# Spike counts accumulated by TensorE in PSUM, and two instead of three tiles for gathered rows

## The chip, the cores and the metric

The kernel runs on one core of one Trainium2 chip. The metric is the device time in microseconds (us) of one execution. The engines are called as the profile calls them: PE (TensorE matmuls; PEld is its weight loads), DVE (VectorE), ACT (ScalarE), POOL (GpSimd) and SP (SyncE).

## The reference

A table of 100001 embeddings of 128 numbers is read at 1024 x 50 positions. For each of 50 steps the running mean of a sequence's rows is normalised over the batch of 1024 and fed to a leaky integrator, whose state v gives off a spike when it reaches 1. The mean number of spikes is multiplied by the whole table.

```python
emb = emb_table.at[0].set(0.0)
e = emb[seq]                                   # (1024, 50, 128)
prefix = jnp.cumsum(e, axis=1)
denom = jnp.minimum(t_idx[None, :], lengths[:, None])
uF = prefix / denom[:, :, None]
y = (uF - uF.mean(axis=0)) * lax.rsqrt(uF.var(axis=0) + BN_EPS) * gamma + beta
def step(v, x):                                # 50 steps
    v = v + (x - v) / 2.0
    spike = (v - 1.0 >= 0)
    return v - spike, spike
_, spikes = lax.scan(step, v0, jnp.moveaxis(y, 1, 0))
scores = spikes.mean(axis=0) @ emb.T           # (1024, 100001): 410 MB
```

## The kernel before

Two stages follow each other: the recurrence over t, then the product with the table, whose 410 MB of results are stored. In the recurrence D = 128 lies on the partitions and the batch on the free axis. Rows are gathered by POOL, 128 rows to an indirect DMA, eight of them to a step (the batch of 1024):

```python
gp = ph.enter_context(tc.tile_pool(name="gather", bufs=3))

def gather(t):
    es[t] = gp.tile([P, B], F32, tag="e", name=f"e_{t}")
    for n in range(NB):                       # NB = 8
        nc.gpsimd.indirect_dma_start(
            out=es[t][:, n * P : (n + 1) * P],
            out_offset=None,
            in_=table,
            in_offset=bass.IndirectOffsetOnAxis(ap=idx[:, n, t : t + 1].bitcast(U32), axis=0),
        )
```

PE transposes them and adds them up in the PSUM banks `pre`; DVE takes the mean and the statistics; ACT scales; DVE does the integrator and counts the spikes:

```python
for t in range(T):                            # T = 50
    last = t == T - 1
    if t + 1 < T:
        gather(t + 1)
    e = es.pop(t)
    # ... (last: s and negv, see below, are made here)
    for h, cs in enumerate(halves):
        for k in range(0, BANK, P):
            nc.tensor.matmul(pre[h][:, k : k + P], lhsT=e[:, ...], rhs=ident, is_transpose=True, ...)
        nc.vector.scalar_tensor_tensor(uF[:, cs], rlen[:, cs], 1.0 / (t + 1), pre[h], ALU.max, ALU.mult)
        nc.vector.bn_stats(bs[:, h, :], uF[:, cs])
    if not last:
        correct(t + 1, l)                     # 2 matmuls into pre, for rows of index 0
    # ... bn_aggr, sqrt and scaling on ACT, five small DVE operations for a
    if t and not last:
        nc.vector.tensor_single_scalar(s, v, V_TH, ALU.is_ge)
    # ...
    if not last:
        x(whole)                              # ACT
        if t:
            nc.vector.tensor_tensor(negv, s, v, ALU.subtract)
        step(whole)                           # DVE: v = -0.5 negv + x
        v = vt
        if t < T - 2:
            spiked(count, whole, v)           # DVE: count = (v >= 1) + count
        # ...
        if T - 8 <= t < T - 2 and t % 2 == 0:
            q = (t - T + 8) // 2
            prepare(0, q, accp.tile([P, HALF], F32, tag="pt", name=f"pt_{q}"))
```

`prepare` transposes a piece of 1024 table rows and splits it into a high and a low part for the product stage. Seven chunks of the table (2 MB each) are loaded at the start, while the recurrence runs. In the product stage each tile of results, 128 x 4096, is stored with one DMA of 2 MB.

## Time and profile before

| | before |
|---|---|
| median of the first 3 runs | 1593.33 us (1592.67 to 1593.39) |
| the profiled execution | 1677.8 us, span 1676.0 us |
| busy, share of the span | PE 63%, DVE 60%, ACT 38%, POOL 23% |
| recurrence, up to the first store | 597.4 us of the profiled span |
| product and stores | 1078.6 us of the profiled span |

The profiled execution was 84.5 us slower than the timed ones. The view of the kernel before in 40 equal slices of 41.9 us gives busy tenths for each engine, then the granted clock of PE and the DMA engines' share in tenths:

```profile
PE   3222322322233378887877887887887878888885
DVE  4677777767776875545555555554555555555553
POOL 7666666666666300000000000000000000000000
PEclk6555555555555589999999999999999999999998
DMA  9311111111111069999999999999999999999998
```

From the third slice to the 14th DVE is busy six to eight tenths and the DMA engines one tenth or less (the 9 and the 3 before them are loads of the table). POOL stands at six tenths. From slice 16 on the DMA engines are full. The chain of work that ended last, by engine:

```profile
DMA 49%; DVE 29%; another core or an unknown queue 7%; PE 7%; ACT 3%; issue 3%; POOL 0%; DVEq 0%; SPq 0%; ACTq 0%
```

### The profile page before, as it was taken

The page shows a single profiled execution, that of the slowest core. Times are in us where ns is not written, and L with a number is a line of the kernel's source. Part 1 is how long each engine was busy: PE and PEld are TensorE (multiplying, and loading weights), DVE is VectorE, ACT ScalarE, POOL GpSimd, SP SyncE. Part 2 cuts the span into 40 slices and gives each one's busy share as a digit, 9 for nine tenths or more (in the row PEclk, how much of TensorE's full clock was granted, in tenths as well). Part 3 has the DMA queues.
Part 4 walks back from the last instruction along what each step waited for, and adds up shares of the span by engine and source line. Part 5 has one row for each costly group of instructions (what it writes and reads, how often), then busy time and mean ns, then how long its engine had stood idle before and what let it go on. Part 6 is the DMA issues. An engine that isn't in the chain of part 4 may idle for free.

```text
span 1676.0 us, 12554 instructions
## 1 busy us (share of the span) xinstructions
PE 1047.9 (63%) x4434; PEld 797.5 (48%) x4434; DVE 999.2 (60%) x1211; ACT 630.2 (38%) x697; POOL 378.3 (23%) x406
## 2 busy tenths in 40 slices
PE   3222322322233378887877887887887878888885
PEld 2111212212222266665666665666665666666664
DVE  4677777767776875545555555554555555555553
ACT  2222222222222244444444444444444444444452
POOL 7666666666666300000000000000000000000000
PEclk6555555555555589999999999999999999999998
DMA  9311111111111069999999999999999999999998
GB/s 341 107 46 46 45 48 48 48 44 49 46 45 46 28 271 419 426 425 419 426 417 419 416 417 417 420 424 414 415 416 415 420 416 423 420 410 418 415 413 352
DMA packets 58411, 488.14 MB, mean 291 GB/s; under 512 B 12491, under 2 KB 13292, under 8 KB 33772
## 3 DMA queue, kind: packets, MB, share of 16 engines
q1 hardware_dynamic: 35728, 424.57, 60.2%
q10 hardware_dynamic: 9820, 36.52, 6.0%
q0 software_dynamic: 12800, 26.24, 5.4%
q8 instruction: 35, 0.57, 0.1%
q14 instruction: 28, 0.23, 0.0%
HBM read 77.69 MB, written 409.60 MB: 291 GB/s over the span
## 4 chain that ended last, share of the span: by engine, by line
DMA 49%; DVE 29%; another core or an unknown queue 7%; PE 7%; ACT 3%; issue 3%; POOL 0%; DVEq 0%; SPq 0%; ACTq 0%
DMA scores<-o 48%; DVE o L403 6%; PE po L148 6%; DVE bs L294 4%; DVE uF L293 4%; DVE v L325 4%; DVE count L263 3%; DVE s L308 3%; DVE negv L330 2%; ACT o L405 2%; ACT v L322 1%; DVE a L316 1%; DMA e<-in_L_rec_emb_table,idx 1%; DVE lo L136 1%
## 5 line engine op out<-in xcount | busy, mean ns | idle before, releaser
L403 DVE TENSOR_SCALAR o<-po 128x1024 f32<-128x1024 f32 x390 | 462.1, 1219 | 448.3 <-DMA scores<-o 356.4
L405 ACT ACTIVATE o<-po 128x1024 f32<-128x1024 f32 (+1 forms) x390 | 384.6, 1018 | 548.3 <-DMA scores<-o 380.9
L187 POOL DMA_INDIRECT e<-in_L_rec_emb_table,idx x400 | 377.6, 944 | 189.3 <-issue 109.5
L148 PE MATMUL po<-hi,countC 128*128 128x512 f32 x784 | 325.7, 416 | 90.0 <-ACT o L405 89.7
L252 PE MATMUL pre<-zT,l 128*128 128x512 f32 x100 | 77.7, 779 | 386.6 <-DVE uF L293 333.9
L148 PE MATMUL po<-lo,countC 128*128 128x512 f32 x784 | 311.5, 398 | 0.0
L148 PE MATMUL po<-hi,countB 128*128 128x512 f32 x588 | 246.9, 420 | 32.7 <-ACT o L405 32.2
L148 PE MATMUL po<-lo,countB 128*128 128x512 f32 x588 | 239.5, 408 | 0.0
L252 PEld LDWEIGHTS pre<-zT,l 128*128 128x128 f32 x100 | 28.8, 289 | 428.8 <-issue 312.8
L148 PEld LDWEIGHTS po<-hi,countC 128*128 128x128 f32 x784 | 150.7, 192 | 151.7 <-ACT o L405 123.0
L148 PEld LDWEIGHTS po<-lo,countC 128*128 128x128 f32 x784 | 150.9, 193 | 27.9
L302 ACT ACTIVATE r<-mv,eps 128x1 f32<-128x1 f32 x50 | 14.8, 295 | 388.5 <-DVE mv L298 229.6
L103 PE MATMUL pt<-ident,rows 128*128 128x128 f32 x782 | 110.0, 286 | 80.9 <-ACT o L405 74.6
L148 PEld LDWEIGHTS po<-hi,countB 128*128 128x128 f32 x588 | 117.5, 200 | 71.8 <-ACT o L405 42.2
L136 DVE TENSOR_TENSOR lo<-pt,hi 128x1024 fp32r<-128x1024 f32 x98 | 117.3, 1216 | 55.3 <-ACT hi L132 55.2
L103 PEld LDWEIGHTS pt<-ident,rows 128*128 128x128 f32 x782 | 92.7, 146 | 107.1 <-ACT o L405 92.8
L293 DVE SCALAR_TENSOR_TENSOR uF<-rlen,pre 128x512 f32<-128x512 f32 x100 | 67.8, 678 | 122.4 <-remote 109.7
L148 PEld LDWEIGHTS po<-lo,countB 128*128 128x128 f32 x588 | 117.2, 199 | 23.6
L132 ACT CAST hi<-pt 128x1024 fp32r<-128x1024 f32 x98 | 98.9, 1009 | 50.8 <-PE pt L103 41.8
L284 PE MATMUL pre<-ident,e 128*128 128x128 f32 x400 | 98.0, 420 | 8.3 <-DMA e<-in_L_rec_emb_table,idx 6.9
L284 PEld LDWEIGHTS pre<-ident,e 128*128 128x128 f32 x400 | 83.9, 222 | 20.4 <-issue 10.5
L148 PE MATMUL po<-hi,countA 128*128 128x512 f32 x194 | 76.6, 395 | 1.1 <-ACT o L405 1.1
(61 smaller groups left out, 679.5 us busy)
## 6 DMA issues: line engine op xcount, KB each, us to landing
scores<-o SPq DMA_DIRECT2D x190, 2048.0 KB
rows<-in_L_rec_emb_table ACTq DMA_DIRECT2D x17, 2048.0 KB
rows<-in_L_rec_emb_table SPq DMA_DIRECT2D x7, 2048.0 KB
scores<-o SPq DMA_DIRECT2D x8, 848.5 KB
e<-in_L_rec_emb_table,idx POOLq DMA_INDIRECT x400
scores<-o SPq DMA_DIRECT2D x2, 1024.0 KB
scores<-o SPq DMA_DIRECT2D x3, 512.0 KB
scores<-o SPq DMA_DIRECT2D x2, 256.0 KB
```

Source lines behind the costliest of these rows:

```text
L103: nc.tensor.transpose(pt[:, k0 : k0 + kw], rows[c][:kw, q * KQ + k0 // P, :], ident[:kw, :kw])
L132: nc.scalar.copy(vh, vp)
L136: nc.vector.tensor_tensor(vl, vp, vh.bitcast(F32), ALU.subtract)
L148: nc.tensor.matmul(po[:, :kw], lhsT=counts[n], rhs=part[:, k0 : k0 + kw], start=j == 0, stop=j == 1,)
L187: nc.gpsimd.indirect_dma_start(out=es[t][:, n * P : (n + 1) * P], out_offset=None, in_=table, in_offset=bass.IndirectOffsetOnAxis(ap=idx[: ...
L252: nc.tensor.matmul(pre[h], lhsT=l, rhs=zT[:, h * BANK : (h + 1) * BANK], start=t == 0, stop=False, skip_group_check=True,)
L284: nc.tensor.matmul(pre[h][:, k : k + P], lhsT=e[:, h * BANK + k : h * BANK + k + P], rhs=ident, start=False, stop=last, is_transpose=True, ...
L293: nc.vector.scalar_tensor_tensor(uF[:, cs], rlen[:, cs], 1.0 / (t + 1), pre[h], ALU.max, ALU.mult)
L294: nc.vector.bn_stats(bs[:, h, :], uF[:, cs])
L325: nc.vector.scalar_tensor_tensor(vt[:, cs], negv[:, cs], -0.5, vt[:, cs], ALU.mult, ALU.add)
L403: nc.vector.tensor_scalar_mul(o[:, h0 : h0 + hw], po[:, :hw], 1.0 / T)
L405: nc.scalar.mul(o[:, h0 : h0 + hw], po[:, :hw], 1.0 / T)
```

## The change

The intent is to take work off DVE, the busiest engine of the recurrence. The spikes `s` are there anyway, as bf16 zeros and ones. PE multiplies them by the identity and adds the result up in two PSUM banks over 49 steps; DVE's count operation goes. To find those two banks, the pieces prepared during the recurrence now use the banks of `v`. The tiles for gathered rows go from three to two. This is the diff, cut to its core:

```diff
-        gp = ph.enter_context(tc.tile_pool(name="gather", bufs=3))
+        gp = ph.enter_context(tc.tile_pool(name="gather", bufs=2))
...
-        count = once.tile([P, B], F32, tag="count", name="count")
-        nc.vector.memset(count, 0.0)
+        ident_h = once.tile([P, P], BF16, tag="ident_h", name="ident_h")
+        nc.vector.tensor_copy(ident_h, ident)
...
+        sums = [accp.tile([P, BANK], F32, tag=f"sums{h}", name=f"sums{h}") for h in range(B // BANK)]
...
+        def counted(t, s):
+            for h in range(B // BANK):
+                nc.tensor.matmul(
+                    sums[h],
+                    lhsT=ident_h,
+                    rhs=s[:, h * BANK : (h + 1) * BANK],
+                    start=t == 0,
+                    stop=t == T - 2,
+                    skip_group_check=True,
+                )
...
             if not last:
                 correct(t + 1, l)
+            else:
+                counted(t - 1, s)
+                count = once.tile([P, B], F32, tag="zT", name="count")
+                for h, cs in enumerate(halves):
+                    nc.scalar.copy(count[:, cs], sums[h])
...
                 nc.vector.tensor_single_scalar(s, v, V_TH, ALU.is_ge)
+                counted(t - 1, s)
...
-                if t < T - 2:
-                    spiked(count, whole, v)
...
-                    prepare(0, q, accp.tile([P, HALF], F32, tag="pt", name=f"pt_{q}"))
+                    prepare(0, q, vp.tile([P, HALF], F32, tag="v1", name=f"pt_{q}"))
...
-        spiked(count, whole, v)
```

(Not shown: the first block of the product stage takes `sums` and the banks of `v` in another order.)

More of the change, by code (lines that the diff above doesn't have):

```diff
@@ L339, in rec_kernel @@
                     q = (t - T + 8) // 2
-                    prepare(0, q, accp.tile([P, HALF], F32, tag="pt", name=f"pt_{q}"))
-        pt = accp.tile([P, HALF], F32, tag="pt", name="pt_3")
+                    prepare(0, q, vp.tile([P, HALF], F32, tag="v1", name=f"pt_{q}"))
+        pt = vp.tile([P, HALF], F32, tag="v0", name="pt_3")
         turned(0, 3, pt)
@@ L365, in rec_kernel @@
         for q in range(1, 4):
-            o = (up if q == 3 else gp).tile([P, HALF], F32, tag="uF" if q == 3 else "e", name=f"o_0_0_{q}")
-            po = (accp if q % 2 == 0 else vp).tile(
-                [P, HALF], F32, tag="v0" if q % 2 else "pt", name=f"po_0_0_{q}"
-            )
-            for k0 in range(0, HALF, BANK):
-                product(po[:, k0 : k0 + BANK], 0, q, 0, k0, BANK)
+            pool, tag = (gp, "e") if q == 1 else (up, "uF")
+            o = pool.tile([P, HALF], F32, tag=tag, name=f"o_0_0_{q}")
+            if q == 1:
+                po = sums
+            else:
+                po = vp.tile([P, HALF], F32, tag=f"v{(q + 1) % 2}", name=f"po_0_0_{q}")
+                po = [po[:, cs] for cs in halves]
             for h, cs in enumerate(halves):
-                if h == 0:
-                    nc.scalar.mul(o[:, cs], po[:, cs], 1.0 / T)
-                else:
-                    nc.vector.tensor_scalar_mul(o[:, cs], po[:, cs], 1.0 / T)
+                product(po[h], 0, q, 0, h * BANK, BANK)
+            nc.scalar.mul(o[:, :BANK], po[0], 1.0 / T)
+            nc.vector.tensor_scalar_mul(o[:, BANK:], po[1], 1.0 / T)
             store(0, q * HALF, o)
```

## The prediction

> **What bounds the kernel now.** I read the busy shares and the 40 slices first, then the stretches, the groups of the recurrence, and the order of time of one step. The slices show two stages: until about 590 us the clock granted to PE is half and the DMA engines are nearly idle (the 50 steps of the recurrence); after that the DMA engines are full (the product and its stores). The sums by stretch, with engines as busy (xinstructions) and then granted clock, DMA share and GB/s:
>
> ```profile
> 60.60:568.10 507.50, 152.06 (x474) 104.21 (x474) 377.67 (x634) 131.77 (x183) 339.53 (x360) 0.51 0.16 47
> ...
> 597.40:1676.00 1078.60, 871.12 (x3883) 676.90 (x3881) 574.37 (x492) 478.34 (x487) 0.00 (x0) 0.97 0.99 414
> ```
>
> The second stretch starts at the first store. DMA is at 0.99 there, and the change leaves its bytes alone, so its 1078.6 us stay. The first stretch is what can move. Its groups, 100 to 540 us:
>
> ```profile
> L187 POOL DMA_INDIRECT e<-in_L_rec_emb_table,idx x309 | 291.5, 943 | 150.0 <-issue 83.9 <-remote 47.9 <-PE pre L252 11.2
> ...
> L263 DVE SCALAR_TENSOR_TENSOR count<-v,count 128x1024 f32<-128x1024 f32 x38 | 46.5, 1224 | 1.5
> ```
>
> DVE is the busiest engine in the recurrence, and the count is one of its long operations. But busy time is not the pace. In order of time (start, duration, engine):
>
> ```profile
> 303.78 0.94 POOL L187 DMA_INDIRECT e<-in_L_rec_emb_table,idx  x1 [0.30 <-issue]
> 304.85 1.22 DVE L263 SCALAR_TENSOR_TENSOR count<-v,count 128x1024 f32<-128x1024 f32 x1
> 305.02 0.94 POOL L187 DMA_INDIRECT e<-in_L_rec_emb_table,idx  x1 [0.30 <-issue]
> 305.99 0.68 DVE L293 SCALAR_TENSOR_TENSOR uF<-rlen,pre 128x512 f32<-128x512 f32 x1
> ...
> 313.60 1.22 DVE L263 SCALAR_TENSOR_TENSOR count<-v,count 128x1024 f32<-128x1024 f32 x1
> ...
> 314.74 0.68 DVE L293 SCALAR_TENSOR_TENSOR uF<-rlen,pre 128x512 f32<-128x512 f32 x1
> ```
>
> A step of DVE without a wait is 314.74 - 305.99 = 8.75 us. A gather is 0.94 us and 0.30 us of issue, one each 1.248 us, and a step needs eight: 9.98 us. **POOL's gathers are slower than DVE's step by 1.23 us even with the count in it.** The trace nevertheless averages 11.3 us a step, because of pauses like this, where DVE and POOL stop together:
>
> ```profile
> 91.37 1.91 PE L284 MATMUL pre<-ident,e 128*128 128x128 f32 x8
> ...
> 104.73 0.69 DVE L293 SCALAR_TENSOR_TENSOR uF<-rlen,pre 128x512 f32<-128x512 f32 x1 [5.78 <-remote]
> ...
> 105.77 0.94 POOL L187 DMA_INDIRECT e<-in_L_rec_emb_table,idx  x1 [5.58 <-remote]
> ```
>
> Both wait for PE's transposes of the same step. PE's records have them over by 93.3 us, yet PE's semaphore counts on only at 104.7; in such pauses it advances in steps of 0.7 us. I hold these for a cost of recording, for a reason of arithmetic. The profiled run took 1677.8 us, the timed ones 1593.33: 84.5 us less. Take the pauses out and let POOL run on: first gather at 3.9 us, 400 x 1.248 = 499.2, so the last ends at 502.8 and not at 568.1 (65.3 less). In the trace the last step's second uF starts at 589.7, because DVE lags; kept fed, it starts 1.3 us (landing, by the gathers' semaphores) and 0.5 us (last transpose) after the last gather, at 504.6. From there to the first store is 7.7 us (589.7 to 597.4), then 1078.6 of stores, and 1.8 by which the profiled run's time exceeds its span: 504.6 + 7.7 + 1078.6 + 1.8 = 1592.7 us. Measured: 1593.33. If DVE paced the timed run, 47 steps of 8.75 from about 40 us would put the last uF near 452 and the total near 1540, which is not what was timed. So the timed kernel is **POOL for 505 us, then the stores**.
>
> **What the Trainium skill says.** "SBUF — State Buffer", section "SBUF: two separate sides": a DVE operation in a two-port mode locks GpSimd out, so it cannot write the descriptors of its DMAs. If the count did that, removing it would speed POOL. The trace says no; the view of the tile e gives minimum, median and maximum in ns:
>
> ```profile
> L187 POOL DMA_INDIRECT e<-in_L_rec_emb_table,idx x400: 938/944/1165, 3.9 to 567.2; - x134
> ```
>
> No gather is stretched while counts run beside it. "Perfetto Trace Analysis", section "DMA Instruction — SWDGE (GPSIMD)": the profiler's end of such a DMA is the end of descriptor generation, not of the movement; agreed, as each landing is signalled about 2.2 us after its issue, after the 0.94 has ended. "TensorE: Matmul & The Clock Gate", section "Wait — 56ns, not 53.3ns?": a cold matmul goes by N / 1.2 GHz, 426.7 ns for 512 columns. The granted clock is 0.51 here, so I use it for the added bf16 matmuls; the kernel before has none to check it on.
>
> **The change, part by part.**
> (a) Removed: 48 counts of 1.22 us in the steps. DVE's step falls from 8.75 to about 7.5 us. 48 x 1.22 = 59 us of DVE work, all beside POOL's 9.98 us a step; on the path: 0.
> (b) Added on PE: 49 x 2 matmuls at some 0.43 us, 42 us in all, beside PE's own 2 x 0.78 + 8 x 0.24 = 3.5 us a step. They stand in PE's queue ahead of the next step's transposes, and wait for s. From the start of a step's second uF: s ends 2.7 us later (307.31 to 310.04), matmuls to 3.8, transposes to 5.8, if the rows are there. DVE asks for the next uF at 6.3, and the last rows come at 9.98. Hidden: 0.
> (c) Two tiles for gathers, not three. gather(t+1) must now wait for the transposes of t-1, not of t-2. Those end about 1.8 us after gather t-1; gather t+1 is due a whole gather (9.98) after that end. Slack 8 us; 0. At the start, while the table rows load, gather 4 is due at 44.0 us and needs transposes of step 2, nominally over at 41.1: still clear.
> (d) Three prepared pieces (t = 42, 44, 46) now use v's banks, so their transposes wait for negv (4.8 us after uF), ACT to 8.0, DVE's lo to 9.2, next second uF near 10.6 against 9.98: some 0.6 us late, three times, each made up in the following step of 7.5 us. 0.
> (e) The end: after the last transposes, two matmuls and two ACT copies of 0.6 us stand ahead of r on ACT. Copies end about 1.75 us after the second uF starts, bs and mv at 1.65: +0.1 us. The old last count (592.64 to 593.86) already lay under the two x of ACT (to 594.41), so its removal gives 0. Product pieces use other PSUM banks; the first stores may gain or lose up to 1 us.
> Sum: about 0. Predicted 1592.5 us.
>
> **The rivals.** (1) DVE bounds the timed run. For it: the chain of waits gives DVE 29% of the span and DMA gathers 1%, and DVE is busiest. Then 48 x 1.22 = 59 us go until POOL's 1592 stops it; but a DVE-paced kernel would already take 1540, so at most pauses of DVE could be regained: 1550 to 1575. Against it: the sum above, off by 0.6 us. (2) PE's late signals are real in timed runs too. Then a signal 10 us late, three tiles deep, is half hidden, and with two tiles POOL stops at almost each of some 20 pauses: 20 x 3 = 60 us more, near 1650. For it: the pauses are in the only trace. Against it: the stores would then have to run some 8% faster unprofiled, with DMA already at 0.99. (3) The count held POOL back through a port: up to 1550; the even 944 ns speaks against it. (4) The store stage starts otherwise, +-3 us.
>
> **Range and chances.** The main sum gives 1592.5; (e) and rival 4 give some 3 us either way. A few late signals or a mild port effect widen it: 1584 to 1602. Faster by over 2% (under 1561.5) needs rival 1 or 3: 0.06. Slower by over 2% (over 1625.2) needs rival 2: 0.07. Within: 0.87.
>
> **What would show it.** The profile after should have gathers still at 944 ns and 1.25 us apart, no count group in the steps but 98 matmuls into sums near 0.43 us, DVE's step near 7.5 us with more idle before uF, and a store stage of 1078 us within 5. The profiled span may well be longer than 1676 (1670 to 1740), since the pauses now stop POOL sooner; the timed runs are what counts. I am wrong if gathers get shorter, if the time falls by 59 us or a large part of it (DVE was the pace), or if timed runs rise by tens of us (two tiles starve POOL).

## The result

| | before | after | ratio |
|---|---|---|---|
| median, 4 runs each | 1593.07 us | 1593.19 us | 1.000 (0.9983 to 1.0018) |

A ratio is taken from the runs, with its 95% interval in brackets; it is not always quite the ratio of the medians quoted. 0.12 us between the medians, and 0.7 us off the predicted 1592.5.

The profile of the changed kernel took 1593.58 us (span 1591.6 us), in line with its timed runs. Its slices are 39.8 us:

```profile
DVE  5777777777777654545555554555555545555553
POOL 6777777777774000000000000000000000000000
DMA  9422222122221999999999999999999999999998
```

The first store comes at 513.4 us where the first profile of the kernel before has it at 597.4. That is no gain: that execution had been slower than the timed ones, and a second profile of the kernel before, below, has its first store at 513.3 us. The chain that ended last now shows POOL:

```profile
DMA 55%; POOL 18%; issue 9%; DVE 9%; PE 7%; ACT 2%; ACTq 0%; DVEq 0%; SPq 0%; POOLq 0%
```

The sums by stretch of the changed kernel, cut at its first and last gather and its first store (busy times of PE, PEld, DVE, ACT and POOL, then clock, DMA share and GB/s):

```profile
4.10:503.60 499.50, 262.94 (x634) 123.63 (x634) 357.37 (x655) 146.34 (x203) 377.93 (x400) 0.52 0.28 82
503.60:513.40 9.80, 5.32 (x16) 3.78 (x17) 7.40 (x15) 5.45 (x8) 0.00 (x0) 0.67 0.03 7
513.40:1591.60 1078.20, 880.73 (x3883) 685.59 (x3881) 574.23 (x492) 479.01 (x488) 0.00 (x0) 0.95 0.99 414
```

The first stretch holds the 400 gathers and nothing but them on POOL: 499.5 us, 1.249 us each. The last is the store stage, 1078.2 us against 1078.6 before. What lies between is 9.8 us. The groups of the changed kernel, from its page, show the gathers unchanged and the new matmuls:

```profile
L187 POOL DMA_INDIRECT e<-in_L_rec_emb_table,idx x400 | 377.9, 945 | 124.3 <-issue 114.5
...
L264 PE MATMUL sums<-s,ident_h 128*128 128x512 bf16 x98 | 49.6, 608 | 61.2 <-DVE s L326 61.2
```

POOL's idle time is 124.3 us, that is 0.30 us ahead of each gather and little else; in the first profile of the kernel before it was 189.3. Here is a stretch of one step of the changed kernel in order of time:

```profile
305.30 0.48 PE L296 MATMUL pre<-ident,e 128*128 128x128 f32 x1 [0.78 <-DMA e<-in_L_rec_emb_table,idx]
305.31 0.94 POOL L187 DMA_INDIRECT e<-in_L_rec_emb_table,idx  x1 [0.30 <-issue]
...
305.81 0.69 DVE L305 SCALAR_TENSOR_TENSOR uF<-rlen,pre 128x512 f32<-128x512 f32 x1 [2.31 <-PE pre L296]
...
307.38 1.17 DVE L326 TENSOR_SCALAR s<-v 128x1024 bf16<-128x1024 f32 x1
...
308.61 1.01 PE L264 MATMUL sums<-s,ident_h 128*128 128x512 bf16 x2 [1.26 <-DVE s L326]
...
315.94 0.69 DVE L305 SCALAR_TENSOR_TENSOR uF<-rlen,pre 128x512 f32<-128x512 f32 x1 [2.55 <-PE pre L296]
```

A step runs from one second uF to the next, 305.81 to 315.94 (10.13 us; the mean over many steps is 9.99). DVE waits 2.3 to 2.6 us in it for PE's transposes, and PE waits for the last of the eight gathers to land (0.78 us before the transpose at 305.30).

### The profile page after: what moved, and what is told of

Same layout as the page of the kernel before. It is cut to its first block, busy times and chain, and to the rows that moved or that the text cites. A ratio compares the mean times of both kernels' runs of the same rounds, so it can differ in the third digit from the quotient of the medians.

```text
span 1591.6 us, 12701 instructions
## 1 busy us (share of the span) xinstructions
PE 1149.0 (72%) x4532; PEld 813.0 (51%) x4532; DVE 940.1 (59%) x1162; ACT 632.1 (40%) x699; POOL 378.6 (24%) x406
## 3 DMA queue, kind: packets, MB, share of 16 engines
q1 hardware_dynamic: 35728, 424.57, 63.4%
## 4 chain that ended last, share of the span: by engine, by line
DMA 55%; POOL 18%; issue 9%; DVE 9%; PE 7%; ACT 2%; ACTq 0%; DVEq 0%; SPq 0%; POOLq 0%
DMA scores<-o 51%; POOL e L187 18%; DVE o L419 7%; PE po L148 5%; DMA e<-in_L_rec_emb_table,idx 4%; ACT o L421 2%; PE pt L103 1%; DVE lo L136 1%; PE pre L296 0%; DVE s L326 0%; DVE bs L306 0%; DVE uF L305 0%; DMA idx<-in_r_seq 0%; ACT v L341 0%; DVEq L419 0%
## 5 line engine op out<-in xcount | busy, mean ns | idle before, releaser
L187 POOL DMA_INDIRECT e<-in_L_rec_emb_table,idx x400 | 377.9, 945 | 124.3 <-issue 114.5
L148 PE MATMUL po<-hi,countC 128*128 128x512 f32 x784 | 333.3, 425 | 90.2 <-ACT o L421 89.7
L148 PE MATMUL po<-lo,countC 128*128 128x512 f32 x784 | 319.0, 407 | 0.0
L296 PE MATMUL pre<-ident,e 128*128 128x128 f32 x400 | 155.0, 449 | 147.3 <-DMA e<-in_L_rec_emb_table,idx 145.7
L148 PEld LDWEIGHTS po<-hi,countC 128*128 128x128 f32 x784 | 155.1, 198 | 154.0 <-ACT o L421 123.6
L296 PEld LDWEIGHTS pre<-ident,e 128*128 128x128 f32 x400 | 79.3, 201 | 241.5 <-DMA e<-in_L_rec_emb_table,idx 219.8
L148 PEld LDWEIGHTS po<-lo,countC 128*128 128x128 f32 x784 | 155.4, 198 | 29.6
L264 PE MATMUL sums<-s,ident_h 128*128 128x512 bf16 x98 | 49.6, 608 | 61.2 <-DVE s L326 61.2
```

Source lines behind the costliest of these rows:

```text
L148: nc.tensor.matmul(po[:, :kw], lhsT=counts[n], rhs=part[:, k0 : k0 + kw], start=j == 0, stop=j == 1,)
L187: nc.gpsimd.indirect_dma_start(out=es[t][:, n * P : (n + 1) * P], out_offset=None, in_=table, in_offset=bass.IndirectOffsetOnAxis(ap=idx[: ...
L264: nc.tensor.matmul(sums[h], lhsT=ident_h, rhs=s[:, h * BANK : (h + 1) * BANK], start=t == 0, stop=t == T - 2, skip_group_check=True,)
L296: nc.tensor.matmul(pre[h][:, k : k + P], lhsT=e[:, h * BANK + k : h * BANK + k + P], rhs=ident, start=False, stop=last, is_transpose=True, ...
```

## The experiments

Eleven runs were made, of the kernel before once more and of ten other kernels, each profiled as well as timed, in 3 rounds unless it is said. Where nothing is said of it, the result was correct.

### The kernel before, profiled again

No edit.

> The kernel before, unchanged, profiled a second time. If the pauses in its first profile (84.5 us over the timed runs) are a matter of that recording, the timed runs are at 1593 us again and the profile may have them or not; a profile without them has the gathers unbroken, 1.25 us apart, the last ending near 503 us, and a span near 1591 us. If the pauses belong to the kernel before (DVE's load or the third tile make them) and the change removed them, this profile has them again, with a span near 1676 us.

Measured: 1593.01 us, ratio 1.000 (0.9983 to 1.0017), and a profile without pauses, span 1591.2 us. Its sums by stretch, cut as those of the changed kernel:

```profile
4.10:503.40 499.30, 240.81 (x538) 104.35 (x538) 417.00 (x703) 146.13 (x203) 377.64 (x400) 0.96 0.28 82
503.40:513.40 10.00, 4.64 (x15) 3.56 (x16) 8.56 (x16) 4.43 (x6) 0.00 (x0) 0.50 0.03 7
513.40:1591.20 1077.80, 874.14 (x3883) 680.11 (x3881) 574.56 (x492) 478.15 (x487) 0.00 (x0) 0.96 0.99 415
```

So the 84.5 us were of that one execution: DVE's load and the third tile are both here, and alone they do not make them. This profile is the one to lay beside that of the changed kernel. DVE's busy time in the gathers' stretch goes from 417.00 to 357.37 us, 59.6 us less, nearly all of it the 48 counts of 1.22 us (58.6). The stretch itself is 499.3 and 499.5 us. Where the 59.6 us went is seen in the waits between 60 and 500 us (waiter, what it waited for: us in all, times, longest), first of the kernel before, then of the changed one:

```profile
DVE uF L293 <- PE pre L284: 41.4, 38, 1.2
```

```profile
DVE uF L305 <- PE pre L296: 94.8, 41, 2.6
```

The mean wait of DVE for the transposed rows rises from 1.1 to 2.3 us, by what the count took. **The freed time became a longer wait for the same gather.**

### The parts of the change, one at a time

Before, with `bufs=2` for the gather pool and nothing else:

```diff
-        gp = ph.enter_context(tc.tile_pool(name="gather", bufs=3))
+        gp = ph.enter_context(tc.tile_pool(name="gather", bufs=2))
```

> The kernel before with two tiles for gathered rows in place of three, the count still on DVE. Theory (POOL's gathers are the pace, a third tile holds nothing that is needed): 1593 us within 2. Rival (two tiles starve POOL, which the lighter DVE of the change made good again): over 1600 us, and in the profile POOL waits on PE's transposes before the first gather of a step.

Measured: 1593.14 us, ratio 1.0001 (0.9984 to 1.0017), gathers unbroken from 4.2 to 503.4 us. The third tile held nothing that was needed, with DVE's full load too.

After, with `bufs=3`, that is the count on PE alone:

> The changed kernel with three tiles for gathered rows, the count on PE. Theory: 1593 us within 2, gathers unbroken. Rival (the count's removal did gain, and two tiles gave it back): clearly under 1593 us, by up to 59 us if DVE had been the pace.

Measured: 1593.65 us, ratio 1.0004 (0.9988 to 1.0021). Neither part gains or loses by itself; the result isn't a gain and a loss that cancel.

### How much slack DVE has

Two operations more of the count's kind and size on DVE in each of 49 steps, the sums going to a tile that nothing reads (it is made and zeroed ahead of the loop):

```diff
                 step(whole)
                 v = vt
+                for _ in range(2):
+                    nc.vector.scalar_tensor_tensor(extra, v, V_TH, extra, ALU.is_ge, ALU.add)
```

In the kernel before:

> The kernel before with two more operations of the count's kind and size on DVE in each of 48 steps (into a tile that nothing reads; results stay right). DVE's step becomes 8.75 + 2.45 = 11.2 us, over POOL's 9.98. Theory: DVE becomes the pace and some 48 x 1.2 = 58 us come on: about 1650 us. If DVE had been the pace already, twice that: 1593 + 48 x 2.45 = 1711 us.

Measured: 1660.77 us, 67.7 over the kernel before. POOL now pauses before the first gather of a step, until PE's transposes have freed a tile:

```profile
300.55 0.94 POOL L187 DMA_INDIRECT e<-in_L_rec_emb_table,idx  x1 [1.46 <-PE pre L286]
301.80 0.94 POOL L187 DMA_INDIRECT e<-in_L_rec_emb_table,idx  x1 [0.30 <-issue]
...
311.69 0.94 POOL L187 DMA_INDIRECT e<-in_L_rec_emb_table,idx  x1 [1.47 <-PE pre L286]
```

A step is 311.69 - 300.55 = 11.14 us, DVE's own 8.75 + 2.4. POOL follows. 48 times 11.14 - 9.99 is 55 us; the rest of the 67.7 comes from what can't be made up any more once DVE is the pace: the steps with a prepared piece (15.6, 12.3 and 12.3 us from one first uF to the next, some 7 us over three plain steps), the last step (12.4 us) and the start, where the kernel before makes up 3 us by which DVE begins late.

In the changed kernel:

> The changed kernel with the same two operations more in each step. DVE's step becomes 7.5 + 2.45 = 9.95 us, just at POOL's 9.98. Theory: 1593 to 1606 us (the three steps with a prepared piece and the first ones can't be made up any more), some 45 to 58 us less than the kernel before with the same load: what the change freed on DVE is there, unused. Rival (DVE was the pace): 48 x 2.45 = 118 us more, 1711 us.

Measured: 1607.08 us, 14.0 us over the kernel before: 1 us past the end of what was expected. About half of it lies in the steps with prepared pieces, which took 14.5, 11.1 and 11.1 us, and most of the rest in the last step (12.4 us) and at the start, as above. Between the two loaded kernels lie 53.7 us. The change frees the 1.2 us a step; they only matter where DVE is the pace.

### Fewer gathers

These two kernels are wrong (relative error 0.56). Six blocks of rows are gathered and two of them are transposed twice, so PE, DVE and ACT have all their work:

```diff
-            for n in range(NB):
+            for n in range(6):
                 nc.gpsimd.indirect_dma_start(
...
-                        lhsT=e[:, h * BANK + k : h * BANK + k + P],
+                        lhsT=e[:, (h * BANK + k) % (6 * P) : (h * BANK + k) % (6 * P) + P],
```

In the kernel before:

> Wrong on purpose: the kernel before gathers six of a step's eight blocks of rows and transposes two of them twice, so that POOL's step is 6 x 1.248 = 7.5 us and all else is as it was. Theory: DVE's 8.75 us becomes the pace, its last uF comes near 451 us and not 505: about 1539 us. If gathers were not the pace, the time stays at 1593 us.

Measured: 1541.61 us, ratio to the kernel before 0.9677 (0.9661 to 0.9693). DVE now runs without waits, from second uF to second uF 8.76 us, and POOL waits for tiles:

```profile
244.70 0.67 DVE L293 SCALAR_TENSOR_TENSOR uF<-rlen,pre 128x512 f32<-128x512 f32 x1
...
248.20 0.94 POOL L187 DMA_INDIRECT e<-in_L_rec_emb_table,idx  x1 [1.57 <-PE pre L284]
...
253.46 0.67 DVE L293 SCALAR_TENSOR_TENSOR uF<-rlen,pre 128x512 f32<-128x512 f32 x1
```

In the changed kernel:

> Wrong on purpose: the changed kernel with six of a step's eight gathers. DVE's step of 7.5 us now meets POOL's 7.5. Theory: here the removed count pays: about 1490 us, some 45 to 55 us (3%) under the kernel before with six gathers. If the two come out alike, something else than DVE's work (a chain through PE and ACT) sets a step's length under POOL's.

Measured: 1485.57 us, ratio to the kernel before 0.9325 (0.931 to 0.9341). A step is 7.49 us, and POOL's six gathers take as much, so the two are level here:

```profile
242.32 0.67 DVE L305 SCALAR_TENSOR_TENSOR uF<-rlen,pre 128x512 f32<-128x512 f32 x1
...
249.81 0.67 DVE L305 SCALAR_TENSOR_TENSOR uF<-rlen,pre 128x512 f32<-128x512 f32 x1
```

With six gathers the same change is worth 1541.61 - 1485.57 = 56.0 us, 3.6%; with eight, nothing. **That the gathers hide the gain is shown, not only argued**: take a quarter of them away and nearly all of it comes out (56.0 of 48 x 1.22 = 59 us).

### A use for the memory that the change frees

The DMA engines are at 0.28 during the recurrence and full afterwards, and 17 whole chunks of the table are read in the full stage. One chunk more loaded ahead needs 16 KB of each partition. The kernel before with eight chunks doesn't build, for want of room for its three gather tiles (they ask for 12 KB of a partition, and 9.8 KB are left). The changed one does, if the product stage gives up memory too. The room that counts is that of the third gather tile: the kernel before with two of them, eight chunks and the second attempt's product stage, below, builds as well, with its count on DVE (it was not run). The first attempt halved the output tiles (5 rounds for each of the four kernels of this part):

```diff
-AHEAD = 7
+AHEAD = 8
...
-            o = op.tile([P, CH], F32, tag="o", name=f"o_{c}_{n}")
             for q in range(-(-w // HALF)):
+                if q % 2 == 0:
+                    o = op.tile([P, 2 * HALF], F32, tag="o", name=f"o_{c}_{n}_{q}")
...                                              (bufs=4; a store of 1 MB after each two q)
```

> A use of what the change freed: with two tiles there is room for an eighth 2 MB chunk of the table to be loaded during the recurrence, when the DMA engines are nearly idle; with three tiles it did not fit. The product stage's output tiles are halved (2048 columns, four of them, 1 MB a store), since its memory must fit too. Theory: the product stage is bound by bytes, 2.1 MB less of them at some 415 GB/s are 5 us: 1588 us. If 1 MB stores or the tighter output tiles cost more than that, 1593 us or above.

Measured: 1615.48 us, ratio 1.0140 (1.0125 to 1.0156): worse. With the halved tiles alone (`AHEAD = 7`, six tiles):

> The changed kernel with halved output tiles alone (2048 columns, six of them, 1 MB a store), seven chunks ahead as before. Tells apart what the eighth chunk and what the halved stores do. Theory: 1593 us within 2, perhaps 1 us less as the first stores can start sooner.

Measured: 1621.20 us, ratio 1.0175 (1.0161 to 1.0189). My expectation of "1593 within 2" was wrong: halving the stores costs 28 us. The queue of the stores moves the same bytes in far more packets. First the changed kernel, then the one with halved stores (queue, kind: packets, MB, share of 16 engines):

```profile
q1 hardware_dynamic: 35728, 424.57, 63.4%
```

```profile
q1 hardware_dynamic: 63088, 424.59, 64.2%
```

In the stretch from 600 to 1000 us the DMA engines are at 1.01 and 1.00, but move 422 and 411 GB/s. The packets of that queue took 63.4% of 1591.6 us and 64.2% of 1618.8 us, that is 1009 and 1039 us: 30 us more for the same bytes, about what the kernel lost. That the number of packets is the reason is not shown by itself, since the size of a store and its bytes in each partition's row were halved together. The two halved kernels are 5.7 us apart. That is not the eighth chunk alone, as it had four output tiles against six; the pair at the end of this part is the clean one.

The second attempt leaves the stores whole and takes the room from the tiles of the split table, five pairs for six:

```diff
-AHEAD = 7
+AHEAD = 8
-        i = order[c, q] % 6
+        i = order[c, q] % 5
...
-                if n == NB - 1 and q < 2:
-                    ready(c + 1, 2 + q)
+                if n == NB - 1 and q < 3:
+                    ready(c + 1, 1 + q)
...
-            if n in (2, 5):
-                ready(c + 1, n // 5)
+            if n == 4:
+                ready(c + 1, 0)
```

> The changed kernel with an eighth chunk of the table loaded during the recurrence and stores whole (2 MB); the room comes from five instead of six pairs of tiles for the split table, so that three pieces instead of two are prepared in the last block of a chunk. Theory: against the changed kernel about 5.7 us less (what the eighth chunk gave with the halved stores: 1621.2 against 1615.5), so 1587.5 us, if the later preparation hides behind the stores. If it doesn't hide, 24 chunks of 1 us or more take the gain: 1593 us or above.

Measured: 1588.30 us (1588.11 to 1589.42), ratio to the kernel before 0.9971 (0.9958 to 0.9985). The last line of its sums by stretch is the store stage, 1073.1 us where the changed kernel has 1078.2 (cut at 513.4 us like that one's; its own first store is at 513.1):

```profile
513.40:1586.50 1073.10, 874.85 (x3882) 679.58 (x3881) 572.04 (x492) 478.32 (x487) 0.00 (x0) 0.96 0.99 414
```

With five pairs and seven chunks:

> The changed kernel with five pairs of tiles for the split table alone, seven chunks ahead as before. Theory: 1593 us within 1. What it is over that is the price of the fifth slot's loss, and the difference to the kernel with eight chunks is what the eighth chunk gives (5 to 6 us).

Measured: 1592.93 us, ratio 0.9998 (0.9984 to 1.0011): the sixth pair was free to give, and the eighth chunk gives 1592.93 - 1588.30 = 4.6 us. So the kernel with eight chunks beats the kernel before by 0.3%; its interval leaves out 1.

## Why the prediction was right

**The bound.** "POOL for 505 us, then the stores" held, and so did its arithmetic. The last gather ended at 503.6 us (put at 502.8: the first began 0.2 later and each took 1.249, not 1.248). From there to the last second uF it was 2.1 us and not 1.8, since landing takes a median 2.5 us from the issue and not 2.2 (the 2.2 was read from a profile that had lost most records of landings, see the next point). Then 7.7 us to the first store and 1078.2 of stores, as put down, and 2.0 us by which the run exceeds its span. The sum of the measured terms is 503.6 + 2.1 + 7.7 + 1078.2 + 2.0 = 1593.6, which is that run's time; they divide it, so the sum must come out. What counts is that each term came within 1 us of the one put down.

**The pauses.** The conclusion that they don't belong to the timed kernel held: a second profile has none, and no other kernel's profile did. The reason that I gave, a cost of recording, isn't shown: the eleven runs of the experiments and the changed kernel were all profiled, and each profiled time lies within 0.1% of its timed runs. One thing speaks for it: the first profile is also the only one that lost records. Its trace holds 7790 updates of semaphores and the second profile of the same kernel 13798, with 12554 instructions in both; of the gathers' landings it holds 1179 of 6400, and its page has no time to landing for any DMA. That the two go together was seen once and proves no cause. What made PE's signals late in that one execution stays open. The step that failed is the last one, that the profiled span after "may well be longer than 1676 (1670 to 1740)": it was 1591.6. I took pauses seen once for a property of every profile.

**(a)** DVE's busy time fell by 59.6 us against the 59 put down, beside POOL, and the path lost nothing. The wait for rows grew from 1.1 to 2.3 us instead.

**(b)** The matmuls: 98 of them, recorded at 608 ns each, but two together span 1.01 us (308.61), so the second starts about 0.4 us after the first, near the 0.43 put down. They ended 3.8 us after the second uF (305.81 to 309.62, estimate 3.8).

**(c)** Two tiles: no gather waited; shown by the kernel before with two tiles, too.

**(d)** The prepared pieces cost no time, but the size was off for the first one. The step's next second uF came 12.0 us after (435.76 to 447.78) and not 10.6, some 2.0 us late against the gathers. The term left out was the zeroing of table row 0, which DVE does behind its step and for which the transposes wait (changed kernel, in order of time):

```profile
442.03 0.17 DVE L100 MEMSET rows<- 1x128 f32 x1
...
442.29 1.94 PE L103 MATMUL pt<-ident,rows 128*128 128x128 f32 x8 [2.73 <-issue]
```

The two others were 0.4 and 0.6 us late. Each was made up in the next step, as put down, thanks to the lighter DVE: in the second profile of the kernel before the first piece left DVE 3 us late, and with the next pieces added it was back on the gathers' pace only at step 48.

**(e)** From the last second uF to the first store it was 7.73 us before (505.57 to 513.30) and 7.73 after (505.75 to 513.48). ACT's r started at 507.42, right after mv, so even the +0.1 us wasn't there.

**The rivals.** DVE as the pace of the timed run is ruled out by the unchanged time, by the two experiments with extra load and by those with six gathers: DVE has 9.99 - 8.75, some 1.2 us a step to spare (an estimate) before it shows. Late signals with two tiles did not occur. A port held by the count is ruled out by the gathers: 945 ns with the count gone, 944 with it.

## What to carry to other kernels

An engine that is busy six tenths can be the pace when its work is many equal pieces with a fixed gap: multiply the start-to-start time by the count before looking at busy shares. Check the profiled time against the timed runs first; where it differs, rebuild the timed time term by term from the profile; an account that misses it has the wrong bound, and one that meets it is still to be tested, as here with fewer gathers. A change that frees an engine off the path is worth something only later: here its DVE time pays once gathers get fewer, and the room of the third tile already paid 0.3%, together with a change of the product stage.

## What the Trainium skill lacked or had wrong

- "DMA: Bandwidth & Descriptors", section "Anatomy of one DMA — SWDGE (gpsimd) path", gives a fit of 2.0 us plus bytes over 436e3 a us for one such DMA; for the 64 KB of a gather that is an estimate of 2.15 us. The runs show 2.4 us at least, 2.5 median and, by run, 6.2 to 7.0 at most from issue to landing. The pace of gathers in a row, 945 ns of descriptor generation and 0.30 us between them (400 in 499.5 us), stands there nowhere that I found, and it was what bounded this kernel's recurrence.
- The same page, section "Measured (HBM→SBUF, 128 partitions, SWDGE, issued from GpSimd)", advises DMAs of 1 MiB and more, for 75% of the peak and up; its table is of loads, and stores are not in it. For the stores here (from SBUF, issued by SP) 1 MB instead of 2 MB cost 28 us in 1593: 63088 packets for 35728, and 411 against 422 GB/s. With the DMA engines full both rates are far above 75% of the larger, so the advice isn't wrong, but 2 MB was worth having.
- No page tells that a single profiled execution can be 84.5 us slower than all others of the same kernel by pauses in which PE's semaphore counts late. It was seen in one of two profiles of the kernel before, the one with 7790 of 13798 semaphore updates in its trace, and in none of the others.
- "TensorE: Matmul & The Clock Gate", section "Seeing it yourself", warns that the trace's events of the clock have been seen to be unreliable. The granted clock in the gathers' stretch is 0.96 in the second profile of the kernel before and 0.52 in that of the changed one, while the median transpose took 475 and 473 ns, and from the start of a step's last gather to its second uF it was 3.1 us in both. So I don't read PE's speed in sparse stretches from that row.
